# A two-layer graph network on one core: a form of its own for the last group, and other places for the first loads and norms

## The chip, the cores and the metric

The kernel runs on one core of a Trainium2 chip. A core has TensorE (matrix products), VectorE (DVE in the profile), ScalarE (ACT), GpSimd (POOL) and SyncE (SP). DMA transfers are issued from the instruction streams of ACT, SP and GpSimd and carried out by sixteen DMA engines. The metric is the device time of one execution in microseconds. The kernel before takes 2562.37 us, the median of three runs (2562.05 to 2563.6).

## The reference

Input `x` is 128 batches of 128 nodes with 512 features, all in float32. Two layers follow one another. Reduced to what is computed:

```python
# layer 0
h = relu(layernorm(x))
q, k, v = h @ Wq.T, h @ Wk.T, h @ Wv.T            # 512 x 512 each
rel = adj.T * (q @ k.T)                           # per batch, 128 x 128
rel = rel / norm(rel, axis=2, keepdims=True)
x = x + rel @ v
# layer 1: 8 heads of 64 columns
h = relu(layernorm(x))
q, k, v = h @ Wq + bq, h @ Wk + bk, h @ Wv + bv
s = q_head @ k_head.T / 8 + where(adj == 0, -1e9, 0)
x = x + concat(softmax(s) @ v_head)
```

## The kernel before

The 128 batches are worked in 32 groups of four (`G = 4`). `Layer0(g)` and `Layer1(g)` hold the two layers of group g. A dense product takes the four batches together: 512 rows by 512 features against a 512 x 512 weight. `Product` (L196) does it by Strassen's way, in seven products of half size, P1 to P7, each of which is four matmuls of 256 columns into one PSUM bank (the profile counts each float32 matmul as two passes, so eight). P1, P5 and P6 end in a copy out of PSUM (L227), P2, P3 and P7 in an addition on DVE (L243), P4 in a copy into the result. The sums of inputs that this needs are `sumA` and `sumB` (L349, L360), the sums of weights are made once (`sums`, L91).

Layer 0 is arranged so that it needs two dense products instead of three: `weights0` (L118) makes Wq' Wk once on TensorE (L124) and copies it out (L115, L116), the product G turns `h` with it (`pg`), `R` (L383) is the relation, `mask_rel` and `square` (L392, L398) mask and square it, `N` and `norms` (L403 to L411) give the norm, `V` (`pv0`) the values, and `O` and `xO` (L415, L421) add the result to `x`. Layer 1 has the dense products Q, K and V, with biases; the scores of one batch, all heads, are `S` (L446); `mk` adds the mask and takes the maximum (L455, L457); `ex` is eight exponentials on ACT with their sums (L464); `A` (L492) is the attention output, with the head's 64 columns as weights, so that it comes out turned (features in the partitions); `oc` copies it out (L503).

Matrices are turned in two ways. The usual one goes through DRAM: `send_blocks` (L182) writes a tile to DRAM in blocks of 32 from ACT's queue, `fetch_blocks` (L188) reads it back with four DMAs from SP's queue so that the blocks lie turned, and DVE turns the inside of each 32 x 32 block. For the norm `h` the three steps are `hn`, `rd` and `T` (L296 to L317), for the exponentials `ex`, `wr` and `wt` (L459 to L482), for the attention output `oc`, `rdo` and `ot` (L499 to L528). `ot` also scales by the reciprocal sums (L520), adds to `x` on GpSimd (L527) and writes the batch out from GpSimd's queue (L528). The other way is on TensorE, with the identity: `hn_pe` and `turn_pe` (L319 to L337), used for group 0 only.

The layernorm is `stat` on DVE (L284, L285), `inv` on GpSimd (four small operations for two batches, L291 to L294) and `hn` on ACT with scale and bias. In each group the two halves of two batches are handled apart: `stat0`, `stat1` and `inv0` serve `hn0`, and so on.

Buffers that matter here: `xpool` 12 tiles of `x`; `npool` ("e", for `hn`, `e` and `oT`) 3; `tpool` ("u", what was read back) 2; `wpool` ("wT") 3; `work` ("o") 2; in PSUM `ps_mm` 4 banks for the products, `ps_s` one double bank for the scores, `ps_o` two banks for everything else.

The order of the work is written out by hand. Under `manual_schedule` (L579) every engine runs its instructions in the order in which the program calls them, and the calls come from strings of steps which `run` (L566) walks through: `FIRST` for group 0, `SECOND` for group 1, `ORDER` for groups 2 to 31, and `LAST` after them. In a step the letter names the object: `m` is layer 0 of the current group, `n` layer 1 of the same group, `f` layer 0 of the next one, `l` and `p` layer 1 of the one before and of the one before that; `w` holds the weights of layer 1. So the pass of group g also carries layer 1 of group g - 1, and `LAST` carries what remains: the last group's Q, K, S, V and A, and the end of the one before.

What comes ahead of the strings (L73 to L74, L98 to L106 and L580 to L592) is the head: the loads of `x` of group 0 from SP's queue (four of 256 KB), of the raw weights of layer 0 from ACT's queue (four pieces of `raw_q` and `raw_k` in turn, 256 KB each, then `raw_v`), then statistics, the loads of group 1 and of layer 1's weights from GpSimd's queue (`load1`, L145, twelve DMAs, of which three carry biases), the turned norm of group 0, `weights0` and `weights_v0`. Of the steps that follow, `w.scale` (L162 to L164) multiplies layer 1's Q weights by 1/8 on ACT.

## Time and profile before

| What | Value |
|---|---|
| median of the runs | 2562.37 us |
| the profiled execution, its own time | 2561.42 us |
| its span, first to last instruction | 2559.6 us |
| PE busy | 2509.3 us, 98% |
| DVE busy | 1714.1 us, 67% |
| ACT busy | 1022.0 us, 40% |
| POOL (GpSimd) busy | 538.1 us, 21% |
| moved by DMA | 409.90 MB, mean 160 GB/s |
| exponentials to DRAM, `d_w<-e` | 128 DMAs of 512 KB, 2.6 us from issue to landing |
| their way back, `u_w<-d_w` | 512 DMAs of 128 KB, 2.9 us |
| attention output to DRAM, `d_o<-oT` | 64 DMAs of 512 KB, 4.2 us |
| its way back, `u_o<-d_o` | 256 DMAs of 128 KB, 3.3 us |

Times in the trace count from the start of the span. In the timeline a line gives the start, the length, the engine and the line of the code, the operation with its tiles and shapes, and in square brackets the idle time before it and what ended it; `x8` means that eight alike instructions stand in one line. An engine's name with a small q is its instruction queue issuing a DMA. In the view by windows a line gives the stretch, then its length, the busy time of PE, PE's weight loads, DVE, ACT and POOL (each with its number of instructions), and at the end three numbers: the clock that TensorE was granted (1.00 is full), the mean busy share of the DMA engines, and GB/s. In the chain of what ended last a line gives start and length of one step; the next line is what it released.

### The profile page before, as it was taken

How to read it: one execution, taken by the hardware profiler on the slowest of the kernel's cores; microseconds unless marked ns; L12 is line 12 of the kernel's file. 1: busy time of each engine (PE TensorE's matmuls, PEld its weight loads, DVE VectorE, ACT ScalarE, POOL GpSimd, SP SyncE). 2: the span in 40 equal slices, each digit the busy share in tenths (PEclk: the TensorE clock that was granted, in tenths of full speed). 3: DMA queues.
4: the chain of work that ended last, by engine and by line, in shares of the span. 5: the costliest groups of instructions: out<-in, count | busy, mean ns of one | idle time of the engine just before them, and what ended most of it. 6: DMA issues, size and time to landing. Idle time of an engine off the chain costs nothing.

```text
span 2559.6 us, 40828 instructions
## 1 busy us (share of the span) xinstructions
PE 2509.3 (98%) x14656; PEld 2131.7 (83%) x14656; DVE 1714.1 (67%) x2485; ACT 1022.0 (40%) x3248; POOL 538.1 (21%) x950
## 2 busy tenths in 40 slices
PE   8999999999999999999999999999999999999994
PEld 5788888888888888888888888888888888888883
DVE  5476766666766667666667666676666767666664
ACT  2344434444433334433444434444334344333442
POOL 4111222122122212122212121111221121222111
PEclk9999999999999999999999999999999999999997
DMA  4255444556444555445555445554445554445543
GB/s 170 83 168 178 161 152 141 181 161 194 152 143 153 179 165 190 146 141 166 173 173 171 152 147 168 169 184 157 148 149 173 165 192 149 146 157 176 162 140 132
DMA packets 374380, 409.90 MB, mean 160 GB/s; under 512 B 29921, under 2 KB 290145, under 8 KB 374177
## 3 DMA queue, kind: packets, MB, share of 16 engines
q1 hardware_dynamic: 281168, 167.92, 23.3%
q10 hardware_dynamic: 71792, 169.89, 17.9%
q0 software_dynamic: 21216, 69.49, 7.6%
q8 instruction: 115, 1.88, 0.3%
q14 instruction: 89, 0.72, 0.1%
HBM read 206.90 MB, written 200.28 MB: 159 GB/s over the span
## 4 chain that ended last, share of the span: by engine, by line
PE 96%; DVE 1%; DMA 1%; ACT 1%; issue 0%; POOL 0%; SPq 0%; ACTq 0%; POOLq 0%; DVEq 0%
PE pv_x L219 17%; PE pq_x L219 9%; PE pv_z L219 9%; PE pk_x L219 9%; PE pg_x L219 9%; PE pss L446 5%; PE po L492 5%; PE pr L383 4%; PE pv_y L219 4%; PE pg_z L219 4%; PE po L415 4%; PE pk_z L219 4%; PE pq_z L219 4%; PE pq_y L219 2%; PE pk_y L219 2%; PE pg_y L219 2%
## 5 line engine op out<-in xcount | busy, mean ns | idle before, releaser
L464 ACT ACTIVATE e<-pss,nmax 128x128 f32<-128x128 f32 x1024 | 359.7, 379 | 202.3 <-DVE nmax L457 180.1
L527 POOL TENSOR_TENSOR xb<-xb,o 128x512 f32<-128x512 f32 x128 | 163.3, 1276 | 1159.3 <-DVE o L520 1157.8
L219 PE MATMUL pv_x<-wc_v,h 128*128 128x256 f32 x1280 | 300.9, 382 | 0.7 <-DVE pv_r L236 0.7
L219 PEld LDWEIGHTS pv_x<-wc_v,h 128*128 128x128 f32 x1280 | 240.4, 190 | 51.6 <-DVE v L243 11.7
L302 ACT ACTIVATE hn<-xb,shift,rstd 128x512 f32<-128x512 f32 x252 | 190.9, 807 | 172.2 <-POOL shift L294 167.4
L219 PE MATMUL pv_z<-wc_v,s 128*128 128x256 f32 x1024 | 245.1, 382 | 0.0
L464 ACT ACTIVATION_READ_ACCUMULATOR e<-pss,nmax 128x1 f32 x1024 | 224.1, 219 | 0.0
L455 DVE TENSOR_TENSOR pss<-pss,mask 128x1024 f32<-128x1024 f32 x128 | 157.1, 1228 | 97.1 <-PE pss L446 97.1
L219 PEld LDWEIGHTS pv_z<-wc_v,s 128*128 128x128 f32 x1024 | 192.1, 190 | 28.5
L314 DVE STREAM_TRANSPOSE h<-u_h 128x1024 f32<-128x1024 f32 x126 | 156.4, 1241 | 86.1 <-DMA u_h<-d_h 78.2
L219 PE MATMUL pv_x<-wc_v,s 128*128 128x256 f32 x768 | 184.9, 384 | 0.0
L219 PE MATMUL pq_x<-h,wc_q 128*128 128x256 f32 x768 | 184.7, 383 | 0.0
L219 PE MATMUL pk_x<-h,wc_k 128*128 128x256 f32 x768 | 181.5, 379 | 0.0
L284 DVE BATCH_NORM_STATS2 st<-xb 128x6 f32<-128x512 f32 x256 | 172.0, 672 | 4.6 <-DMA xb<-in_x_dram 4.6
L446 PEld LDWEIGHTS pss<-kT,qT 64*128 64x128 f32 x2048 | 124.3, 187 | 49.4 <-PE po L415 23.5
L291 POOL TENSOR_SCALAR rstd<-mv 128x2 f32<-128x2 f32 x128 | 28.4, 221 | 650.3 <-DVE mv L285 650.3
L219 PEld LDWEIGHTS pq_x<-h,wc_q 128*128 128x128 f32 x768 | 143.4, 190 | 23.4 <-ACT oT L503 5.1
L219 PEld LDWEIGHTS pk_x<-h,wc_k 128*128 128x128 f32 x768 | 145.9, 190 | 19.9
L479 DVE STREAM_TRANSPOSE wT<-u_w 128x1024 f32<-128x1024 f32 x128 | 152.8, 1194 | 10.4 <-DMA u_w<-d_w 10.4
L457 DVE TENSOR_REDUCE nmax<-pss 128x8 f32<-128x1024 f32 x128 | 156.7, 1224 | 4.4
L219 PEld LDWEIGHTS pv_x<-wc_v,s 128*128 128x128 f32 x768 | 140.8, 190 | 20.4 <-DVE pv_r L236 0.2
L446 PE MATMUL pss<-kT,qT 64*128 64x128 f32 x2048 | 149.0, 285 | 3.1 <-ACT e L464 2.9
(134 smaller groups left out, 4440.4 us busy)
## 6 DMA issues: line engine op xcount, KB each, us to landing
d_w<-e ACTq DMA_DIRECT2D x128, 512.0 KB, 2.6
u_w<-d_w SPq DMA_DIRECT2D x512, 128.0 KB, 2.9
d_h<-hn ACTq DMA_DIRECT2D x126, 512.0 KB, 3.5
u_h<-d_h SPq DMA_DIRECT2D x504, 128.0 KB, 3.2
d_o<-oT ACTq DMA_DIRECT2D x64, 512.0 KB, 4.2
u_o<-d_o SPq DMA_DIRECT2D x256, 128.0 KB, 3.3
out_dram<-xb POOLq DMA_DIRECT2D x128, 256.0 KB, 2.9
xb<-in_x_dram POOLq DMA_DIRECT2D x124, 256.0 KB, 3.2
```

What stands on the lines that cost most here:

```text
L219: nc.tensor.matmul(ps[:, m, :], lhsT=lhsT, rhs=rhs, start=first and m == 0 and k == 0, stop=k == 1, skip_group_check=True,)
L284: nc.vector.bn_stats(st, x_tiles[g, b])
L302: nc.scalar.activation(hn[:, r], x_tiles[g, b].rearrange("p (k j q) -> p j k q", j=TB, q=BK), AF.Relu, bias=self.shift[:, b : b + 1], scal ...
L314: nc.vector.transpose(half.rearrange("p k (t i) -> p t k i", i=BK), self.u.pop(i).rearrange("p t (k q) -> p t k q", q=BK),)
L383: nc.tensor.matmul(pr[:, b, :], lhsT=self.turned(k, b), rhs=self.gT[:, k, ts(b, P)], start=(k == 0), stop=(k == KD - 1),)
L446: nc.tensor.matmul(pss[:, r, k, :], lhsT=self.qT[rows, k, ts(b, P)], rhs=self.kT[rows, k, ts(b, P)], start=True, stop=True,)
L455: nc.vector.tensor_tensor(sc, sc, mask[:, None, :].to_broadcast([P, H, P]), ALU.add)
L457: nc.vector.tensor_reduce(self.nmax[b], sc, AX.X, ALU.max, negate=True)
L464: nc.scalar.activation(e[:, :, i, :], sc[:, i, :].rearrange("p (j q) -> p j q", q=BK), AF.Exp, bias=nmax[:, i : i + 1], accum_out=self.tot ...
L479: nc.vector.transpose(self.wT[b].rearrange("p h (t i) -> p t h i", i=BK), self.uw.pop(b).rearrange("p t (h q) -> p t h q", q=BK),)
L492: nc.tensor.matmul(po[r * HD : (r + 1) * HD, k, :], lhsT=self.v[:, b, ts(2 * k + r, HD)], rhs=wT[:, r * NH + k, :], start=True, stop=True,)
L527: nc.gpsimd.tensor_tensor(xb, xb, o.rearrange("p k t q -> p (k t q)"), ALU.add)
```

## The change

The change has two parts, which share no step.

**The head.** The four loads of group 0's `x` are issued from SP's queue behind `raw_k`, which itself moves from ACT's queue to SP's; `raw_q` stays on ACT's. The object `f` (layer 0 of group 1) is made before `weights0`, and its statistics (`f.stat` for four batches, on DVE) and `f.inv0`, `f.inv1` (on GpSimd) stand right behind `m.hn_pe(1)`, ahead of the copies of `pa` on DVE and behind the DMA issues of group 1's loads and of `load1` on GpSimd. In `FIRST` these steps are gone; `f.hn0 f.rd0` stand right behind `m.G.P1`, `w.scale` behind `m.G.P5`, `m.V.P4` ahead of `n.hn0`, `n.hn1 n.rd1` behind `f.G.P5` and `n.T0` behind `f.G.P7`.

**The last group.** `LAST` is new from `l.Q.P3` on. `p.A1 p.oc1 p.rdo1` stand behind `l.S1 l.mk1`. Batches 0 and 1 of the last group keep the exponentials' way through DRAM. Batches 2 and 3 have `mk` and `ex` in halves of four heads (`mkA`, `mkB`, `exA`, `exB`); `e` is written in plain order and turned on TensorE by `tw` (eight transposes into two PSUM tiles of `ps_o`, each copied out on ACT). All four batches have their attention output from `An`: eight matmuls with the turned exponentials as weights and 64 columns of `v` as the moving side, so that it comes out with the nodes in the partitions. `fin` multiplies it by the reciprocal sums on DVE, adds it to `x` (on GpSimd, for batch 3 on DVE) and writes it out from SP's queue. For this group there is no `oc`, `rdo` and `ot`. `p.ot1`, the end of the group before, stands between `fin1` and `fin2`.

```diff
...
         queue.dma_start(xb, x[g * G + b])
         x_tiles[g, b] = xb
-    for b in range(G):
-        load(0, b, nc.sync)
     ident = const.tile([P, P], F32, tag="ident", name="ident")
     make_identity(nc, ident)
...
     for name, w, tag in (("q", wq0, "pq"), ("k", wk0, "pk"), ("v", wv0, "pv0")):
         raw[name] = ppool.tile([P, KD, D], F32, tag=tag, name=f"raw_{name}")
     for k in range(KD):
-        for name, w in (("q", wq0), ("k", wk0)):
-            nc.scalar.dma_start(raw[name][:, k, :], w[ts(k, P), :])
+        for name, w, queue in (("q", wq0, nc.scalar), ("k", wk0, nc.sync)):
+            queue.dma_start(raw[name][:, k, :], w[ts(k, P), :])
+    for b in range(G):
+        load(0, b, nc.sync)
     nc.scalar.dma_start(raw["v"], wv0.rearrange("(k p) d -> p k d", p=P))
     adj_sb = const.tile([P, P], F32, tag="adj", name="adj_sb")
     nc.sync.dma_start(adj_sb, adj)
...
             self.kT = ppool.tile([P, NH, G * P], F32, tag="pk", name=f"kT_{g}")
             self.Q = Product(self, "q", self.qT, True, bq_sb, name=f"pq_{g}")
             self.K = Product(self, "k", self.kT, True, bk_sb, name=f"pk_{g}")
-            self.rs, self.wT, self.ps, self.nmax, self.po = {}, {}, {}, {}, {}
+            self.rs, self.wT, self.ps, self.nmax, self.po, self.e = {}, {}, {}, {}, {}, {}
             self.dw, self.uw, self.total, self.do, self.uo = {}, {}, {}, {}, {}
         def start_v(self):
...
                 self.wT[b].rearrange("p h (t i) -> p t h i", i=BK),
                 self.uw.pop(b).rearrange("p t (h q) -> p t h q", q=BK),
             )
+        def mk_r(self, b, r):
+            sc = self.ps[b][:, r * NH : (r + 1) * NH, :]
+            nc.vector.tensor_tensor(sc, sc, mask[:, None, :].to_broadcast([P, NH, P]), ALU.add)
+            if r == 0:
+                self.nmax[b] = small.tile([P, H], F32, tag="nmax", bufs=2, name=f"nmax_{self.g}_{b}")
+            nc.vector.tensor_reduce(
+                self.nmax[b][:, r * NH : (r + 1) * NH], sc, AX.X, ALU.max, negate=True
+            )
+        def ex_r(self, b, r):
+            g, sc, nmax = self.g, self.ps[b], self.nmax[b]
+            if r == 0:
+                self.total[b] = small.tile([P, H], F32, tag="total", bufs=4, name=f"total_{g}_{b}")
+                self.e[b] = npool.tile([P, H, P], F32, tag="e", name=f"en_{g}_{b}")
+            for i in range(r * NH, (r + 1) * NH):
+                nc.scalar.activation(
+                    self.e[b][:, i, :], sc[:, i, :], AF.Exp,
+                    bias=nmax[:, i : i + 1], accum_out=self.total[b][:, i : i + 1],
+                )
+        def tw(self, b):
+            g = self.g
+            self.wT[b] = wpool.tile([P, H, P], F32, tag="wT", name=f"wT_{g}_{b}")
+            for r in range(2):
+                pt = ps_o.tile([P, NH, P], F32, tag="po", name=f"pw_{g}_{b}_{r}")
+                for k in range(NH):
+                    nc.tensor.transpose(pt[:, k, :], self.e[b][:, r * NH + k, :], ident)
+                nc.scalar.copy(self.wT[b][:, r * NH : (r + 1) * NH, :], pt)
+            self.rs[b] = small.tile([P, H], F32, tag="rs", bufs=8, name=f"rs_{g}_{b}")
+            nc.vector.reciprocal(self.rs[b], self.total.pop(b))
+        def An(self, b):
+            po, wT = ps_o.tile([P, D], F32, tag="po", name=f"pn1_{self.g}_{b}"), self.wT.pop(b)
+            for r in range(2):
+                for k in range(NH):
+                    i = 2 * k + r
+                    nc.tensor.matmul(
+                        po[:, ts(i, HD)], lhsT=wT[:, r * NH + k, :], rhs=self.v[:, b, ts(i, HD)],
+                        start=True, stop=True,
+                    )
+            self.po[b] = po
+        def fin(self, b):
+            g, xb = self.g, x_tiles.pop((self.g, b))
+            o = work.tile([P, D], F32, tag="o", name=f"o_{g}_{b}")
+            nc.vector.tensor_tensor(
+                o.rearrange("p (k r d) -> p k r d", k=NH, r=2),
+                self.po.pop(b).rearrange("p (k r d) -> p k r d", k=NH, r=2),
+                self.rs.pop(b).rearrange("p (r k) -> p k r", r=2)[:, :, :, None].to_broadcast(
+                    [P, NH, 2, HD]
+                ),
+                ALU.mult,
+            )
+            (nc.vector if b == G - 1 else nc.gpsimd).tensor_tensor(xb, xb, o, ALU.add)
+            nc.sync.dma_start(out[g * G + b], xb)
...
         def A(self, i):
...
     FIRST = """
-        m.sumA m.sumB m.start m.G.P1 w.scale m.G.P2 f.stat0 f.stat1 f.inv0 m.G.P5 f.hn0 f.rd0 m.G.P6 w.sumq
-        m.G.P3 f.stat2 f.stat3 f.inv1 m.V.P1 f.hn1 f.rd1 w.sumv m.G.P7 m.V.P2 w.sumk m.G.P4 m.V.P5
+        m.sumA m.sumB m.start m.G.P1 f.hn0 f.rd0 m.G.P2 m.G.P5 w.scale m.G.P6 w.sumq m.G.P3 m.V.P1 f.hn1 f.rd1
+        w.sumv m.G.P7 m.V.P2 w.sumk m.G.P4 m.V.P5
         m.R m.mask_rel m.square f.T0 m.V.P6 m.V.P3 m.N m.norms m.V.P7 m.O0 m.xO0 m.O1 m.xO1 n.stat0 n.stat1
-        n.inv0 n.hn0 n.rd0 m.V.P4 f.T1 m.O2 m.O3 f.sumA f.start f.G.P1 m.xO2 m.xO3 n.stat2 n.stat3 n.inv1
-        n.hn1 n.rd1 f.G.P2 f.sumB f.G.P5 f.G.P6 f.G.P3 n.T0 f.G.P7 f.G.P4 n.T1 n.start
+        n.inv0 m.V.P4 n.hn0 n.rd0 f.T1 m.O2 m.O3 f.sumA f.start f.G.P1 m.xO2 m.xO3 n.stat2 n.stat3 n.inv1
+        f.G.P2 f.sumB f.G.P5 n.hn1 n.rd1 f.G.P6 f.G.P3 f.G.P7 n.T0 f.G.P4 n.T1 n.start
     """.split()
     SECOND = """
         l.Q.P1 l.sumA l.Q.P2 l.sumB l.K.P1 l.K.P2 l.Q.P5 l.Q.P6 f.load0 f.load1 l.Q.P3 l.K.P5 l.K.P6 l.Q.P7
...
         l.wr3 l.V.P3 l.V.P7 n.T0 l.A0 l.oc0 l.V.P4 n.T1 n.start
     """.split()
     LAST = """
-        l.Q.P1 p.rdo0 l.sumA l.Q.P2 l.sumB l.K.P1 l.K.P2 p.wt3 l.Q.P5 p.ot0 l.Q.P6 l.Q.P3 p.A1 p.oc1
-        p.rdo1 l.K.P5 l.K.P6 l.Q.P7 l.K.P3 l.S0 l.mk0 l.K.P7 l.Q.P4 l.ex0 l.wr0 l.K.P4 l.S1 l.mk1 p.ot1
-        l.start_v l.V.P1 l.V.P2 l.ex1 l.wr1 l.V.P5 l.S2 l.mk2 l.V.P6 l.ex2 l.wr2 l.V.P3 l.wt0 l.V.P7 l.S3 l.mk3
-        l.V.P4 l.ex3 l.wr3 l.wt1 l.A0 l.oc0 l.rdo0 l.wt2 l.wt3 l.A1 l.oc1 l.rdo1 l.ot0 l.ot1
+        l.Q.P1 p.rdo0 l.sumA l.Q.P2 l.sumB l.K.P1 l.K.P2 p.wt3 l.Q.P5 p.ot0 l.Q.P6 l.Q.P3 l.K.P5 l.K.P6 l.K.P3
+        l.Q.P7 l.S0 l.mk0 l.K.P7 l.Q.P4 l.ex0 l.wr0 l.K.P4 l.S1 l.mk1 p.A1 p.oc1 p.rdo1 l.start_v l.V.P1
+        l.ex1 l.V.P2 l.V.P5 l.S2 l.mkA2 l.mkB2 l.V.P6 l.exA2 l.exB2 l.wt0 l.wr1 l.V.P3 l.V.P7 l.S3 l.mkA3 l.mkB3
+        l.tw2 l.wt1 l.exA3 l.exB3 l.V.P4 l.An0 l.fin0 l.An1 l.fin1 p.ot1 l.tw3 l.An2 l.fin2 l.An3 l.fin3
     """.split()
     def run(order, **who):
...
         load1()
         m.hn_pe(0)
         m.hn_pe(1)
+        f = Layer0(1)
+        for b in range(G):
+            f.stat(b)
+        f.inv(0)
+        f.inv(1)
         weights0(lambda: m.turn_pe(0))
         m.turn_pe(1)
         weights_v0()
         for g in range(NG):
             n = Layer1(g)
-            f = Layer0(g + 1) if g + 1 < NG else None
+            if g:
+                f = Layer0(g + 1) if g + 1 < NG else None
             run((FIRST, SECOND, ORDER)[min(g, 2)], p=p, l=l, m=m, n=n, f=f, w=Weights1())
             p, l, m = l, n, f
         run(LAST, p=p, l=l)
```

More of the change, by code (lines that the diff above doesn't have):

```diff
@@ L484, in A, with mkA, mkB, exA @@
+        def mkA(self, b):
+            self.mk_r(b, 0)
+        def mkB(self, b):
+            self.mk_r(b, 1)
+        def exA(self, b):
+            self.ex_r(b, 0)
+        def exB(self, b):
+            self.ex_r(b, 1)
         def A(self, i):
```

## The prediction

> **What bounds the kernel now.** First the page's engine shares and the line of 40 slices, to see whether any engine is full and where it is not:
>
> ```profile
> PE 2509.3 (98%) x14656; PEld 2131.7 (83%) x14656; DVE 1714.1 (67%) x2485; ACT 1022.0 (40%) x3248; POOL 538.1 (21%) x950
> ...
> PE   8999999999999999999999999999999999999994
> ```
>
> TensorE is the bound; only the first and the last slice are open. Taking the start of each group's first Q product from the timeline, groups 1 to 31 follow each other every 77.57 us (one 77.63), with no TensorE wait in between. So whatever moves the head moves the end by the same amount, and there are two places to look: before group 0's Q (at 85.55 us) and after the last dense product. The head, from the TensorE and ACT timelines:
>
> ```profile
> 34.41 1.89 PE L219 MATMUL pv_x<-wc_v,h 128*128 128x256 f32 x8
> 41.31 3.56 PE L219 MATMUL pg_x<-s,wc_a 128*128 128x256 f32 x8 [5.00 <-ACT pg_r L227]
> ...
> 61.37 1.89 PE L219 MATMUL pv_x<-wc_v,h 128*128 128x256 f32 x8
> 68.67 3.77 PE L415 MATMUL po<-v,rel 128*128 128x512 f32 x4 [5.41 <-ACT v L227]
> ```
> ```profile
> 38.64 1.52 ACT L302 ACTIVATE hn<-xb,shift,rstd 128x512 f32<-128x512 f32 x2 [6.90 <-POOL shift L294]
> ...
> 66.02 1.52 ACT L302 ACTIVATE hn<-xb,shift,rstd 128x512 f32<-128x512 f32 x2 [9.93 <-POOL shift L294]
> 67.56 0.37 ACTq L185 DMA_DIRECT2D d_h<-hn  x1
> 68.03 0.58 ACT L227 COPY v<-pv_x 128x512 f32<-128x512 f32 x1 [0.49 <-ACT hn L302]
> ```
>
> Both TensorE stalls have one form: TensorE needs a small ACT copy (`pg_r`, `v`), and that copy stands in ACT's queue behind a norm (`hn`) which waits for GpSimd's `shift`. After each stall the products run at half speed (3.56 instead of 1.89 for eight), and the windows view shows the granted clock (the first of the last three numbers) fall with it; the last row is the tail:
>
> ```profile
> 40.00:50.00 10.00, 8.69 (x32) 7.33 (x33) 6.08 (x9) 3.34 (x6) 6.01 (x8) 0.83 0.45 157
> 60.00:70.00 10.00, 4.59 (x14) 2.72 (x13) 6.21 (x10) 2.10 (x3) 1.73 (x4) 0.77 0.14 54
> 2530.00:2540.00 10.00, 3.68 (x32) 2.91 (x29) 3.03 (x4) 1.17 (x2) 0.23 (x1) 0.50 0.57 171
> ```
>
> The tail, from the chain that ended last (start, length, what):
>
> ```profile
> 2528.24 2.60 DMA d_w<-e
> ...
> 2532.30 3.29 DMA u_w<-d_w
> ...
> 2537.21 1.99 PE po L492 x16
> 2539.22 0.59 ACT oT L503
> 2539.83 2.70 DMA d_o<-oT
> ...
> 2543.95 3.12 DMA u_o<-d_o
> ...
> 2552.47 0.58 POOLq L625
> ```
>
> The exponentials (`d_w`, `u_w`) and then the output (`d_o`, `u_o`) each go through DRAM to be turned: write, four issues, read, about 7.5 us each time.
>
> **The head, step by step.** By queue: raw_k goes to SP beside raw_q on ACT, and x(0) behind raw_k. The Trainium skill (DMA: Bandwidth & Descriptors, "Issuing engines are not separate DMA queues") says that a second issuing queue saves only issue time, as all share 16 engines. That speaks against any gain here: with doubled bandwidth x(0) would be in by about 9. The trace agrees with the rule: the first eight transfers (2 MB) landed by 8.58 from two queues, and from one queue 256 KB then took 0.65 each. So x(0), now after 2 MB of weights and sharing with raw_v, lands at 9.8 to 13.7 instead of 4.6 to 8.2. Then statistics 0.9, `inv` 1.6 on GpSimd: to 16.2 (was 10.8). What is late next is x(1), queued on GpSimd behind that `inv`: issue to landing 3.0 for the first (median of these loads on the page 3.2; 3.8 here under load), then 0.55 to 0.65 each: 19.2 to 21.1. The added `f.stat` of four tiles (about 0.8 each) now stand on DVE ahead of the copies of `pa`: done at 22.5. The copies started at 20.78 before. 8 x 0.43 gives 26.0, and the transposes of raw_v, which wait for them, let the first G product begin at 26.4 (25.78 before): **+0.6**. TensorE itself starts at about 4.9 (6.14 before) and has done pa and the turns by 22.9, so it is not what binds.
>
> `f.inv` on GpSimd stands behind sixteen DMA issues (12.0 long before, of which 1.2 waits): 16.2 + 11 = 27.2, done 28.9 and 30.4. `f.hn0` runs on ACT 28.9 to 30.4, right after G.P1's copy; the P5 copy is due only at 31.8, so ACT holds nobody. `w.scale` (2.3) then ends at 34.7 and G.P6's copy at 35.3; G.P7 needs it at 36.8. The 5.00 stall and its half-clock product (3.35 between starts instead of 1.73) go. Ten products of 1.727 from 26.4 put R at 43.7 (50.00 before): **-6.3** so far.
>
> R to V.P4's end is 13.2 by its rows. V.P4's copy now precedes `n.hn0` on ACT: 0.16 drain, 0.1 and 0.58, so O2 starts at 57.7 (68.67): 4.7 more. O2 and O3 at full clock take 1.73 rather than 3.57: 1.8 more. From there six G products, the wait for P7's addition (0.85, stays), G.P4: Q.P1 at 72.6 instead of 85.55. **Head: -12.9.**
>
> What could now be late: `n.hn1` has moved behind G.P5's copy (65.4), so hn1's write is issued at 67.0. Its write took 6.23 before (x(2) loads were in flight; 2.75 alone), the read 4.0, the turn and sum 2.0: ready at 79.3; Q.P5 wants it at 79.5. The cover is 0.2, and beyond it each us late costs one. x(2) loads still go off just before, so the 6.2 stands. The T0 chain ends at about 71.7, under Q.P1's 72.6.
>
> Clock: the skill (TensorE: Matmul & The Clock Gate, Parts 1 and 4) says that about 3.4 us of idling halve the clock and that transposes do not count as busy. Between 22.9 and 26.4 TensorE has only raw_v's transposes (1.75). The rows show half clock after idles of 5.0 and 5.4, none after 2.0 (at 2506.67). By the rule the head would lose 1.7 more (-11.2), by the rows nothing; I take the rows, and the other for the range.
>
> **The tail, step by step** (before's time, the head's shift left out). Without p.A1 (1.9) between the products, Q.P4 starts at 2498.3 and ex0 runs 2500.9 to 2503.8, 2.8 earlier; S1 2503.9; p.A1 2505.0; V.P1, P2, P5 to 2512.1. ex1 has ended by 2511.0, behind p.oc1's copies, so S2 starts at once (2513.48 before). The head halves: mask 128x512 like the 0.69 of L392, reduction the same (half of L457's 1.22 plus its fixed part; between 0.61 and 0.75). Four in a row take 2.9 where two took 2.5: +0.4, and in the built order the exponentials wait for the second half's maximum, so halving hides nothing. ex2 2516.3 to 2519.2, S3 2519.2, the eight turns at 0.109 (row of L336) to 2521.2, V.P4 to 2523.0. An is not in the trace: sixteen passes of 64 columns on 128-column weights. Below it lies L492, 0.9 for 64-column weights; the nearest row is L403, 0.11 a pass with full weights and one column: 1.75. I take 1.7; at half clock up to 3.4. An0 to 2524.7. wT1's read waits for wT0's buffer, since u_o of the previous group holds the other: SP 2518.3, landed 2522.8, turned after mk3 at 2524.9. An1 to 2526.7; ex3 2523.4 to 2526.3; tw3 to 2528.1, copies 0.58; An2 2529.8, An3 2531.5.
>
> Next the moved p.ot1. It takes 2.8 of DVE and, on GpSimd, two additions (1.27) with two DMA issues (0.30 + 0.56) between fin1 and fin2, and both `o` buffers. GpSimd: fin0, fin1 to 2529.0, p.ot1 to 2533.5, fin2 to 2534.8. fin3's multiply waits for the last `o` buffer (2532.6), its addition is on DVE (to 2534.0). SP issues the last two rows by 2535.7, landing at 2538 (2.3 to 2.6). The program's end followed the last GpSimd issue by 7.1 before (2552.5 to 2559.6): from the issue at 2532.9 that gives 2540.0, from fin2's end 2541.9. I take 2541. **Tail: -18.6** (-15 to -20.5). Two DRAM trips, 15 us, and the last GpSimd row are gone; p.ot1 gives some 3 back.
>
> The sum is against the profiled execution: span 2559.6 - 12.9 - 18.6 = 2528.1, execution 2561.42 - 31.5 = 2529.9; the median of the runs lies 0.95 above that execution, so 2562.37 - 31.5 = **2531**.
>
> **Rivals.** *Head eaten by late data* (0.14): loads at 0.8 instead of 0.65 per 256 KB, or hn1's write queued wholly behind x(2), hold G.P1 and Q.P5 some 3 to 6 longer: head -8, 2536. For it: two covers under 1 us. *Tail held by GpSimd and cold clock* (0.10): An at 3.4 and `o` buffers in turn: tail -13, 2537. *More than the sum* (0.07): G.P1 at 25.5 and an end without GpSimd's trail: 2525. *The change does nothing, as the stalls move* (0.02): both ACT copies again behind norms: the head and the tail's gain would both have to fail. *Slower* (0.03): one window of 3.41 at half clock in every group costs 1.7 x 31 = 53, 2584; it decides from 1.05 lost per group (31.5 / 30). Against it: no TensorE wait in any group, and groups 1 to 30 keep their orders and their waits. *My forecast* (0.64).
>
> **How the numbers follow.** The likeliest case spans 2527 to 2535. The first two rivals end at about 2540, the faster one at 2524; with these the range holds the 8 in 10. About 0.2% (5 us) is what can be told from no change: faster needs a sixth of the sum, 0.95; same 0.02; slower 0.03.
>
> **What would show it.** Right: no wait for ACT at 36 and 63; granted clock 1.00 between 30 and 80; Q.P1 near 72.6; no `d_w` and `d_o` of the last two batches; about 55 us from the last group's Q.P1 to the end of the last An (62.7 before: 2476.5 to 2539.2), and p.ot1's two additions between fin1 and fin2 on GpSimd. Wrong: a DVE wait for xb longer than to 21, a TensorE wait for `h` or `s` at group 0's Q.P5, or group times other than 77.57.

## The result, and the profile after

The changed kernel takes 2538.26 us (median of five runs, 2536.59 to 2540.92), the kernel before 2562.37 in the same comparison: a ratio of 0.9907, with a 95% interval of 0.9892 to 0.9921. That is 24.1 us less; the forecast was 31.5 less. The profiled execution, which is the median run, has a span of 2536.5, so 23.1 below the 2559.6 of before and 8.4 above the 2528.1 that the prediction's sum gave.

The page of the changed kernel, its engine shares and the lines of 40 slices:

```profile
PE 2512.7 (99%) x14672; PEld 2135.8 (84%) x14672; DVE 1707.5 (67%) x2484; ACT 1023.9 (40%) x3248; POOL 535.0 (21%) x945
...
PE   8999999999999999999999999999999999999998
...
PEclk9999999999999999999999999999999999999999
```

The last slice, which was 4 before, is now 8: the end is filled with matrix work. The start of each group's first Q product splits the span into three. Before, group 0's came at 85.55, the last group's at 2476.5, and 83.1 us followed. Now they come at 76.75 and 2469.5, and 67.0 us follow. So the head gave 8.8, of which 1.7 was lost again inside group 0; the groups after it follow each other every 77.57 as before; and the tail gave 16.1. The head in the timeline of TensorE (start, length, what, and in brackets the idle time before it and what ended it):

```profile
25.20 3.31 PE L139 MATMUL pwv<-ident,raw_v 128*128 128x128 f32 x16 [2.53 <-issue]
28.30 2.62 PE L218 MATMUL pg_x<-h,wc_a 128*128 128x256 f32 x8
...
44.22 1.99 PE L218 MATMUL pg_x<-h,wc_a 128*128 128x256 f32 x8 [1.22 <-DVE gT L242]
...
61.71 1.98 PE L414 MATMUL po<-v,rel 128*128 128x512 f32 x4 [0.68 <-ACT v L226]
...
76.75 1.89 PE L218 MATMUL pq_x<-h,wc_q 128*128 128x256 f32 x8
...
84.83 1.99 PE L218 MATMUL pq_z<-s,wc_q 128*128 128x256 f32 x8 [1.02 <-DVE qT L242]
```

The two stalls that the prediction set out to remove are gone: 5.00 us ahead of `pg_x<-s` is nothing, and 5.41 ahead of the second `po` is 0.68. But four smaller losses have come: 2.53 ahead of the turns of raw_v (`pwv`), which then take 3.31 instead of 1.91; a first G product of 2.62; 1.22 ahead of G.P4; and 1.02 ahead of Q.P5. The windows (length, busy time of PE, weight loads, DVE, ACT, POOL; then granted clock, DMA share, GB/s):

```profile
20.00:30.00 10.00, 7.39 (x34) 5.43 (x33) 8.62 (x22) 3.66 (x10) 8.69 (x13) 0.83 0.97 336
...
40.00:50.00 10.00, 8.78 (x50) 7.66 (x50) 7.76 (x9) 2.76 (x5) 5.25 (x4) 1.00 0.33 105
...
60.00:70.00 10.00, 9.32 (x39) 7.14 (x38) 8.91 (x17) 3.74 (x6) 4.03 (x9) 1.00 0.20 72
...
2490.00:2500.00 10.00, 8.00 (x52) 6.83 (x52) 3.97 (x4) 4.48 (x20) 0.00 (x0) 0.88 0.13 53
```

The clock is whole where it had fallen (40 to 50, 60 to 70) and falls at two other places: 20 to 30, and 2490 to 2500. At the end the chain shows what has taken the place of the trip of the output through DRAM:

```profile
2526.81 1.28 POOL xb L597
...
2528.12 0.70 DVE o L531
...
2528.84 1.95 DVE xb L539
```

GpSimd's addition for `p.ot1` (L597) holds an `o` buffer, then DVE multiplies the last batch and adds it in 1.95 us.

### The profile page after: what moved, and what is told of

The parts are those of the page before. It is cut to its first block, busy times and chain, and to the rows that moved or that the text cites. A ratio compares the mean times of both kernels' runs of the same rounds, so it can differ in the third digit from the quotient of the medians.

```text
span 2536.5 us, 40820 instructions
## 1 busy us (share of the span) xinstructions
PE 2512.7 (99%) x14672; PEld 2135.8 (84%) x14672; DVE 1707.5 (67%) x2484; ACT 1023.9 (40%) x3248; POOL 535.0 (21%) x945
## 3 DMA queue, kind: packets, MB, share of 16 engines
q1 hardware_dynamic: 278992, 167.92, 23.4%
## 4 chain that ended last, share of the span: by engine, by line
PE 97%; DVE 1%; DMA 1%; ACT 0%; issue 0%; POOL 0%; SPq 0%; ACTq 0%; DVEq 0%; POOLq 0%
PE pv_x L218 18%; PE pq_x L218 9%; PE pv_z L218 9%; PE pk_x L218 9%; PE pg_x L218 8%; PE pss L445 5%; PE po L562 5%; PE pv_y L218 5%; PE pg_z L218 4%; PE pq_z L218 4%; PE pr L382 4%; PE pk_z L218 4%; PE po L414 4%; PE pk_y L218 2%; PE pg_y L218 2%; PE pq_y L218 2%
## 5 line engine op out<-in xcount | busy, mean ns | idle before, releaser
L597 POOL TENSOR_TENSOR xb<-xb,o 128x512 f32<-128x512 f32 x124 | 158.2, 1276 | 1103.6 <-DVE o L590 976.4
```

The lines of the kernel that those rows point to most:

```text
L597: nc.gpsimd.tensor_tensor(xb, xb, o.rearrange("p k t q -> p (k t q)"), ALU.add)
```

## The experiments

The theory after reading the two traces: the change does what it says, and the missing 8 us are four separate losses, each with its own cause: (1) group 0's `x` behind 2 MB of weights, and the clock that falls in the idle time which that makes; (2) DVE slowed by GpSimd's additions ahead of G.P4; (3) a PSUM bank that is freed late, ahead of Q.P5; (4) idle time ahead of S1 in the last group, and half clock after it. The rivals: the parts act on each other (the head changes what the tail meets); the loads are bound by the DMA engines, so that no other order helps; every repair only uncovers the next wait.

### One part alone

The first run has the order `LAST` of before, the second the head and `FIRST` of before.

> The new head with the old last group. By the difference of the two profiled executions the new head is worth 6.9 us at the last group's first Q product (2476.5 to 2469.6), and the old tail then runs as it did before, 83.1 us from there to the end: span about 2552.7, 6 to 7.5 below before. The prediction on record gave the head 12.9 (2547). If the two parts help each other (the end of the head changing what the tail meets), the sum of this run and the one with the tail alone will miss the 23 to 24 of both together by more than 2.

> The old head with the new last group. From the last group's first Q product the changed kernel needs 66.9 us where before needed 83.1: span about 2543.4, 16.2 below before; the prediction on record gave 18.6. Where the wait for S1 falls decides whether the clock is halved after it: full clock throughout would give 1.9 more, 18.

Measured: the head alone 2555.82 us, 0.9976 (0.9965 to 0.9987) of before's 2562.02; the tail alone 2543.97, 0.9929 (0.9914 to 0.9944). That is 6.2 and 18.1, together 24.3, and both parts together gave 24.1: the parts add up. The tail's profiled execution beat its expectation by 0.7 (span 2542.7) since the clock stayed whole in it; from its last group's first Q product it needed 65.4 us, not 67.0.

### Where the head's gain lies

```diff
-        n.inv0 m.V.P4 n.hn0 n.rd0 f.T1 m.O2 m.O3 f.sumA f.start f.G.P1 m.xO2 m.xO3 n.stat2 n.stat3 n.inv1
+        n.inv0 n.hn0 n.rd0 m.V.P4 f.T1 m.O2 m.O3 f.sumA f.start f.G.P1 m.xO2 m.xO3 n.stat2 n.stat3 n.inv1
```

> The changed kernel with one step of FIRST moved back: m.V.P4 behind n.hn0 n.rd0 as before. V.P4's copy on ACT then stands behind the norm that waits for GpSimd's shift: the copy comes at about 65.8 instead of 61.1, O2 starts at 66.4 instead of 61.7, with some 5 us of idle TensorE ahead of it and half clock after it. First Q product at 82 to 83 (75.1 to 78.3 with this head in three executions), of which 1 is given back at Q.P5; the whole 4 to 5.5 us longer than the changed kernel, about 2543. If the copy's place is not what the head gains from, under 1.

Measured: 2542.12 us, 3.9 above the changed kernel's median. TensorE's timeline has the old stall back, half clock after it included:

```profile
68.07 3.78 PE L414 MATMUL po<-v,rel 128*128 128x512 f32 x4 [5.35 <-ACT v L226]
```

The first Q product came at 85.31, later than the 82 to 83 expected, since G.P4 and the product behind it ran at half clock in this execution. Group 0 was 1.6 shorter, as the wait at Q.P5 was gone. So the first Q product came 7 to 10 later than in the other runs with the changed kernel's head, and where it came before the change (85.55). The time says the same: 0.9922 of before, beside 0.9929 with the tail alone, which differ by less than the noise. Without this one copy's move, what the other edits of the head win at the first stall goes to the losses that they bring. No run moves this copy alone in the old head, so what it gives by itself is not shown.

### Group 0's loads

```diff
     for k in range(KD):
         for name, w, queue in (("q", wq0, nc.scalar), ("k", wk0, nc.sync)):
             queue.dma_start(raw[name][:, k, :], w[ts(k, P), :])
-    for b in range(G):
-        load(0, b, nc.sync)
+        for b in range(2 * k, min(2 * k + 2, G)):
+            load(0, b, nc.sync)
```

> The changed kernel with SP's first issues in another order: raw_k 0, x 0 and 1, raw_k 1, x 2 and 3, raw_k 2 and 3. My reading of the changed kernel is that x of group 0 behind 2 MB of weights makes everything that follows it late (inv1 ends at 16.8 instead of 10.8, x of group 1 lands to 23.3, the statistics end at 24.4 where the copies of pa could start at 20.8), and that TensorE's 2.5 us without work then halves its clock. So here inv1 ends at about 11, the statistics by 19, the copies start as pa ends, G.P1 starts at 24.4 to 25.0 (28.3 in the changed kernel) at full clock, and the first Q product at 72 to 73 (76.75): 4 us less. The rival is that the 16 DMA engines are the limit: raw_k then comes later by what x gains, pa ends about 2 us later, and G.P1 starts no earlier than 27.

Measured: 2533.67 us, 0.9889 (0.9875 to 0.9904) of before. TensorE's timeline:

```profile
21.71 2.66 PE L139 MATMUL pwv<-ident,raw_v 128*128 128x128 f32 x16
24.20 1.89 PE L218 MATMUL pg_x<-h,wc_a 128*128 128x256 f32 x8
...
31.93 1.99 PE L218 MATMUL pg_z<-s,wc_a 128*128 128x256 f32 x8 [0.66 <-ACT pg_r L226]
...
41.59 3.55 PE L218 MATMUL pg_x<-h,wc_a 128*128 128x256 f32 x8 [2.49 <-DVE gT L242]
```

G.P1 starts at 24.20, without idle time ahead of the turns and at full clock. The rival of the DMA engines falls: raw_k's last piece landed at 13.5 instead of 8.5, and yet `pa` ended at 20.9 instead of 21.8. But the first Q product is only 0.9 earlier than in the changed kernel, not 4. G.P3 (31.93) waits for P5's copy, which now comes late behind `f.hn0`: GpSimd's `f.inv0` ended at 29.28, just ahead of the product P5 (29.55), and `hn0` then held ACT:

```profile
29.31 1.52 ACT L301 ACTIVATE hn<-xb,shift,rstd 128x512 f32<-128x512 f32 x2 [2.59 <-POOL shift L293]
...
31.29 0.59 ACT L226 COPY pg_r<-pg_z 128x512 f32<-128x512 f32 x1 [0.46 <-PE pg_x L218]
```

And G.P4's wait has grown to 2.49, and that product runs at half clock (3.55). (The time is 4.6 below the changed kernel's median. Of the 2.6 between the two profiled executions 0.9 comes from the head and 1.6 from the tail, whose clock stayed whole here.) The rival "it uncovers the next wait" holds here until loss 2 and the place of `f.hn0` are mended too.

### DVE beside GpSimd

```diff
-        w.sumv m.G.P7 m.V.P2 w.sumk m.G.P4 m.V.P5
-        m.R m.mask_rel m.square f.T0 m.V.P6 m.V.P3 m.N m.norms m.V.P7 m.O0 m.xO0 m.O1 m.xO1 n.stat0 n.stat1
+        m.G.P7 m.V.P2 w.sumk m.G.P4 m.V.P5
+        m.R m.mask_rel m.square f.T0 m.V.P6 m.V.P3 m.N m.norms w.sumv m.V.P7 m.O0 m.xO0 m.O1 m.xO1 n.stat0 n.stat1
```

> The changed kernel with w.sumv, four additions on GpSimd, moved from behind hn1 to behind m.norms; nothing on DVE is moved. In the changed kernel the four DVE instructions of w.sumq take 1.00, 1.64, 1.77 and 1.75 while GpSimd adds, where the same on w.sumk takes 0.69 as soon as GpSimd is done; they hold G.P3's addition and so G.P4 by 1.2 us (2.5 and then half clock in the kernel with x between). If GpSimd's additions slow DVE's, then those of sumq that start after GpSimd's sums of v0 take 0.69, sumq ends at least 1.5 us earlier, and G.P4 does not wait; first Q product 1.4 to 3 earlier than with the same head. If they are slow for themselves, nothing changes at G.P4.

First the changed kernel's DVE: three of `w.sumq`'s four, the addition of G.P3 that they hold, and two of `w.sumk`'s, of which the first still meets GpSimd's last addition (it ends at 45.3) and the second does not:

```profile
37.96 1.64 DVE L91 TENSOR_TENSOR wc_q<-wc_q 128x512 f32<-128x512 f32 x1
39.52 1.77 DVE L92 TENSOR_TENSOR wc_q<-wc_q,w_q 128x512 f32<-128x512 f32 x1
41.21 1.75 DVE L93 TENSOR_TENSOR wc_q<-wc_q 128x512 f32<-128x512 f32 x1
42.89 0.68 DVE L242 TENSOR_TENSOR gT<-pg_z,pg_r 128x512 f32<-128x512 f32 x1
...
44.69 1.18 DVE L90 TENSOR_TENSOR wc_k<-w_k,wc_k 128x512 f32<-128x512 f32 x1
45.91 0.69 DVE L91 TENSOR_TENSOR wc_k<-wc_k 128x512 f32<-128x512 f32 x1
```

Then the four of `w.sumq` in the run with `w.sumv` moved, where GpSimd's last sum of v0 runs from 38.0 to 39.8:

```profile
37.96 0.69 DVE L90 TENSOR_TENSOR wc_q<-w_q,wc_q 128x512 f32<-128x512 f32 x1 [3.48 <-ACT w_q L162]
38.69 1.64 DVE L91 TENSOR_TENSOR wc_q<-wc_q 128x512 f32<-128x512 f32 x1
40.25 0.68 DVE L92 TENSOR_TENSOR wc_q<-wc_q,w_q 128x512 f32<-128x512 f32 x1
40.85 0.68 DVE L93 TENSOR_TENSOR wc_q<-wc_q 128x512 f32<-128x512 f32 x1
```

The same instructions, on the same tiles, take 0.68 once GpSimd is silent and 1.64 beside it. G.P4 did not wait, and V.P2 to R took 5.18 instead of 6.67. The additions out of PSUM (42.89, with GpSimd busy) kept their 0.68. The Trainium skill (SBUF — State Buffer, "SBUF: two separate sides") names a cause: GpSimd and DVE share a pair of SBUF ports, held as a lock for a whole instruction, and a DVE instruction with two inputs in SBUF needs it beside a GpSimd one that reads SBUF. The rows agree with it, and GpSimd is slowed too: its addition beside these took 1.79 instead of 1.28. The lock itself stands in no row. The whole was 2535.52 us. Its profiled execution, the longest of the four, reached the first Q product only at 77.21: it had 4.19 us idle ahead of raw_v's turns, with half clock behind them, and lost 1.0 there against the changed kernel, and 0.9 in a new wait for `h` ahead of Q.P1.

### The bank ahead of Q.P5

```diff
-        f.G.P2 f.sumB f.G.P5 n.hn1 n.rd1 f.G.P6 f.G.P3 f.G.P7 n.T0 f.G.P4 n.T1 n.start
+        f.G.P2 f.sumB f.G.P5 n.hn1 n.rd1 f.G.P6 f.G.P3 f.G.P7 n.T0 f.G.P4 n.start
...
-        l.Q.P1 l.sumA l.Q.P2 l.sumB l.K.P1 l.K.P2 l.Q.P5 l.Q.P6 f.load0 f.load1 l.Q.P3 l.K.P5 l.K.P6 l.Q.P7
+        l.Q.P1 l.Q.P2 l.T1 l.sumA l.sumB l.K.P1 l.K.P2 l.Q.P5 l.Q.P6 f.load0 f.load1 l.Q.P3 l.K.P5 l.K.P6 l.Q.P7
```

> The changed kernel with n.T1 of group 0 moved from FIRST into SECOND behind Q.P2, so that on DVE Q.P2's addition comes ahead of the turn of the second half, not behind it and sumA. In the changed kernel Q.P5 waits 1.02 us: not for s, which is ready at 83.45, but for a PSUM bank, which that addition frees at 84.78. If that is so, Q.P5 follows K.P2 with no more than 0.2 us of wait, and the first group takes 64.3 instead of 65.45. If s was what was late, nothing is won.

Measured: Q.P5 (`pq_z`) follows K.P2 (`pk_y`) without a wait:

```profile
80.10 1.89 PE L218 MATMUL pk_y<-h,wc_k 128*128 128x256 f32 x8
81.83 1.89 PE L218 MATMUL pq_z<-s,wc_q 128*128 128x256 f32 x8
```

Group 0 takes 63.72 us instead of 65.45, as it did before the change. The time was 2536.6: 1.7 below the changed kernel, as it should be, but less than the runs of that kernel differ among themselves.

### The hole ahead of S1

```diff
-        l.Q.P7 l.S0 l.mk0 l.K.P7 l.Q.P4 l.ex0 l.wr0 l.K.P4 l.S1 l.mk1 p.A1 p.oc1 p.rdo1 l.start_v l.V.P1
+        l.Q.P7 l.S0 l.mk0 l.K.P7 l.Q.P4 l.ex0 l.wr0 l.K.P4 p.A1 p.oc1 p.rdo1 l.S1 l.mk1 l.start_v l.V.P1
```

> The changed kernel with p.A1, p.oc1, p.rdo1 ahead of S1 instead of behind it. In the changed kernel TensorE has nothing for 2.0 us ahead of S1 and then runs S1 and p.A1 at half clock (1.65 and 3.02 instead of 1.1 and 1.9). If the idle 2.0 us halves the clock, p.A1 in that hole keeps the clock at 1.00 from 2490 to 2510, and V.P1 starts 3.4 us earlier after the last group's first Q product (32.1 us in the changed kernel, 28.7 here); the end comes 3 to 3.5 us earlier. If the clock falls for another reason, only the 1.9 of the hole are gained.

TensorE in the changed kernel, S1, p.A1 and V.P1:

```profile
2497.09 1.65 PE L445 MATMUL pss<-kT,qT 64*128 64x128 f32 x16 [2.00 <-ACT e L463]
2498.67 3.09 PE L562 MATMUL po<-wT,v 128*64 128x128 f32 x32
2501.69 1.99 PE L218 MATMUL pv_x<-wc_v,h 128*128 128x256 f32 x8
```

and with p.A1 in the hole:

```profile
2496.70 1.97 PE L562 MATMUL po<-wT,v 128*64 128x128 f32 x32
2498.76 1.16 PE L445 MATMUL pss<-kT,qT 64*128 64x128 f32 x16
2499.86 1.99 PE L218 MATMUL pv_x<-wc_v,h 128*128 128x256 f32 x8
```

V.P1 came 28.7 us behind the last group's first Q product, as expected, the clock stayed whole, and the end came at 63.8 instead of 67.0. The median, 2537.12, is only 1.1 lower; in the profiled execution the head was 1.5 later at the first Q product, and 1.5 of the 3.2 are left at the end.

The other runs tell more about this hole than the one made for it. It is there, 2.0 us long, in ten of the profiles. In five of them (before, the tail alone, x between, V.P4 back, the output turned) S1 took 1.16 and the clock stayed whole; in five (the changed kernel, the head alone, sumv later, Q.P2 first, the exponentials in DRAM) the clock fell, at S1 or at what follows it. So 2.0 us of idle time halve the clock in some executions and not in others, for 1.6 us (65.4 or 67.0 to the end in the kernels whose tail is the changed one's). The Trainium skill (TensorE: Matmul & The Clock Gate, Part 1, "What's actually happening") says that activity is judged in windows of 3.4 us that run freely, and that the clock falls after an idle one. The profiles show such windows: in each of them the granted clock changes only on a grid of 3.41 us, and the grid lies differently in every run. In the five profiles in which the clock fell, the whole hole lies in one window of the grid, in which TensorE was busy for 1.41 to 1.45 us. In the other five an edge of the grid cuts the hole, no window is left with less than 1.51, and the clock stays whole. The window with the hole and the one behind it, in the changed kernel and then with the tail alone:

```profile
2494.19:2497.60 3.41, 1.41 (x13) 0.96 (x13) 0.00 (x0) 2.94 (x18) 0.00 (x0) 1.00 0.01 2
2497.60:2501.01 3.41, 3.41 (x34) 3.19 (x34) 2.14 (x2) 1.07 (x3) 0.00 (x0) 0.50 0.43 163
...
2503.31:2506.72 3.41, 1.83 (x30) 1.71 (x32) 0.57 (x1) 2.36 (x12) 0.00 (x0) 1.00 0.31 129
2506.72:2510.13 3.41, 3.41 (x34) 2.99 (x30) 2.11 (x3) 2.23 (x9) 0.00 (x0) 1.00 0.46 132
```

So where the hole falls decides, as the page has it; but the window need not be idle throughout, since 1.45 us of work in it were too little. Ahead of G.P4 the border is about the same: windows with 1.53 or less were followed by half clock, those with 1.71 or more were not. (With only An to do, at the very end, up to 2.5 us of work were too little; why, no run tells.) Ahead of raw_v's turns, six profiles have a window with 0.40 to 1.07 us of work, and the clock fell in all six, after 2.53 us of idle time or more. With 1.87 or less it stayed whole, also where a window held nothing but 2.07 or 2.10 us of these turns (Q.P2 first, the head alone).

### Which half of the new last group pays

The exponentials of batches 2 and 3 through DRAM:

```diff
-        l.ex1 l.V.P2 l.V.P5 l.S2 l.mkA2 l.mkB2 l.V.P6 l.exA2 l.exB2 l.wt0 l.wr1 l.V.P3 l.V.P7 l.S3 l.mkA3 l.mkB3
-        l.tw2 l.wt1 l.exA3 l.exB3 l.V.P4 l.An0 l.fin0 l.An1 l.fin1 p.ot1 l.tw3 l.An2 l.fin2 l.An3 l.fin3
+        l.ex1 l.V.P2 l.V.P5 l.S2 l.mk2 l.V.P6 l.ex2 l.wt0 l.wr1 l.V.P3 l.V.P7 p.ot1 l.wr2 l.S3 l.mk3
+        l.wt1 l.ex3 l.wr3 l.V.P4 l.An0 l.fin0 l.An1 l.fin1 l.wt2 l.An2 l.fin2 l.wt3 l.An3 l.fin3
```

> The last group with its attention output in rows (An, fin) as in the changed kernel, but with the exponentials of batches 2 and 3 turned through DRAM as before (whole mk and ex, wr, wt), and p.ot1 behind V.P7, since a read-back buffer comes free only with it. By the rows of the changed kernel: p.ot1 to 2518.4, mk3 to 2520.9, ex3 to 2524, the write to 2526.7, the read to 2530, the turn to 2531.3, An3 to 2533.2, its row at 2534.7 instead of 2530.8: 3.5 to 4 us longer, a span of about 2540. The rival: with the output in rows the way of the exponentials through DRAM is hidden, and the span stays within 1 of 2536.5.

The output turned:

```diff
-        l.tw2 l.wt1 l.exA3 l.exB3 l.V.P4 l.An0 l.fin0 l.An1 l.fin1 p.ot1 l.tw3 l.An2 l.fin2 l.An3 l.fin3
+        l.tw2 l.wt1 l.exA3 l.exB3 l.V.P4 l.A0 l.oc0 p.ot1 l.rdo0 l.tw3 l.A1 l.oc1 l.rdo1 l.ot0 l.ot1
```

> The changed kernel with the exponentials of batches 2 and 3 turned on TensorE as in it, but the last group's attention output as before: turned (A), copied (oc), through DRAM (rdo) and turned back (ot), with p.ot1 behind oc0. By the rows: A1 ends at 2526, oc1's copies at 2527.3, the write at 2530, the read at 2534, ot1 on DVE and GpSimd at 2538 to 2539 and the last row out by 2545: 8 to 10 us longer than the changed kernel, about 2547. With the 5.0 of the run that kept the exponentials in DRAM these make up the 16 to 18 of the tail only if A1, S1 and the end of the previous group bring the rest; if this run is under 5 longer, the row form of the output is not where the tail's gain lies.

Measured: 2543.5 us with the exponentials in DRAM, 2550.22 with the output turned. To the end they need 71.95 (beside the 67.0 of the changed kernel, both with the clock fallen) and 76.46 (beside 65.4, both with it whole): 4.9 and 11.0. TensorE in the first of them, the last two outputs:

```profile
2526.09 3.65 PE L522 MATMUL pn<-v,wT 128*128 128x64 f32 x16 [2.15 <-DVE wT L478]
2531.89 3.65 PE L522 MATMUL pn<-v,wT 128*128 128x64 f32 x16 [2.15 <-DVE wT L478]
```

Each waits for the turn of what came back from DRAM, and each takes 3.65 instead of 1.8: waiting brings the half clock with it, which the 3.5 to 4 had left out. The output in rows is the larger half. Together they are 15.9 of the 17.7 by which the tail gets shorter where its clock stays whole (83.1 to 65.4); the rest, p.A1's place and the end of the group before among it, no run separates.

### All repairs together

The first of three, against the run with `x` between:

```diff
-        m.sumA m.sumB m.start m.G.P1 f.hn0 f.rd0 m.G.P2 m.G.P5 w.scale m.G.P6 w.sumq m.G.P3 m.V.P1 f.hn1 f.rd1
-        w.sumv m.G.P7 m.V.P2 w.sumk m.G.P4 m.V.P5
-        m.R m.mask_rel m.square f.T0 m.V.P6 m.V.P3 m.N m.norms m.V.P7 m.O0 m.xO0 m.O1 m.xO1 n.stat0 n.stat1
+        m.sumA m.sumB m.start m.G.P1 w.scale m.G.P2 m.G.P5 f.hn0 f.rd0 m.G.P6 m.G.P3 m.V.P1 f.hn1 f.rd1
+        m.G.P7 m.V.P2 w.sumq w.sumk m.G.P4 m.V.P5
+        m.R m.mask_rel m.square f.T0 m.V.P6 m.V.P3 m.N m.norms w.sumv m.V.P7 m.O0 m.xO0 m.O1 m.xO1 n.stat0 n.stat1
...
-        f.G.P2 f.sumB f.G.P5 n.hn1 n.rd1 f.G.P6 f.G.P3 f.G.P7 n.T0 f.G.P4 n.T1 n.start
+        f.G.P2 f.sumB f.G.P5 n.hn1 n.rd1 f.G.P6 f.G.P3 f.G.P7 n.T0 f.G.P4 n.start
...
-        l.Q.P1 l.sumA l.Q.P2 l.sumB l.K.P1 l.K.P2 l.Q.P5 l.Q.P6 f.load0 f.load1 l.Q.P3 l.K.P5 l.K.P6 l.Q.P7
+        l.Q.P1 l.Q.P2 l.T1 l.sumA l.sumB l.K.P1 l.K.P2 l.Q.P5 l.Q.P6 f.load0 f.load1 l.Q.P3 l.K.P5 l.K.P6 l.Q.P7
...
-        l.Q.P7 l.S0 l.mk0 l.K.P7 l.Q.P4 l.ex0 l.wr0 l.K.P4 l.S1 l.mk1 p.A1 p.oc1 p.rdo1 l.start_v l.V.P1
+        l.Q.P7 l.S0 l.mk0 l.K.P7 l.Q.P4 l.ex0 l.wr0 l.K.P4 p.A1 p.oc1 p.rdo1 l.S1 l.mk1 l.start_v l.V.P1
```

> The changed kernel with all the repairs together: x of group 0 between the pieces of raw_k, w.scale back ahead of f.hn0 (which goes behind G.P5's copy), w.sumq behind V.P2's addition, w.sumv behind m.norms, Q.P2's addition ahead of T1, p.A1 ahead of S1. If the losses are what I take them for and lie one behind the other, G.P1 starts at 24.2, the first Q product at 70.5 to 71 (76.75 in the changed kernel) without a wait over 0.7 on the way but for O2's and G.P4's, the first group takes 63.7, and the end is 63.8 behind the last group's first Q product: a span of 2525.5, a time of 2527. If each repair only moves the wait to the next cover, the span stays above 2530.

The second, against the first:

```diff
-        l.ex1 l.V.P2 l.V.P5 l.S2 l.mkA2 l.mkB2 l.V.P6 l.exA2 l.exB2 l.wt0 l.wr1 l.V.P3 l.V.P7 l.S3 l.mkA3 l.mkB3
-        l.tw2 l.wt1 l.exA3 l.exB3 l.V.P4 l.An0 l.fin0 l.An1 l.fin1 p.ot1 l.tw3 l.An2 l.fin2 l.An3 l.fin3
+        l.ex1 l.V.P2 l.V.P5 l.S2 l.mk2 l.V.P6 l.exA2 l.exB2 l.wt0 l.wr1 l.V.P3 l.V.P7 l.S3 p.ot1 l.mk3
+        l.tw2 l.wt1 l.exA3 l.exB3 l.V.P4 l.An0 l.fin0 l.An1 l.fin1 l.An2 l.fin2 l.tw3 l.An3 l.fin3
```

> As combo_a, with the last group's mk whole again (2.45 instead of 2.88 for four halves), p.ot1 ahead of mk3 instead of between fin1 and fin2, and An2, fin2 ahead of tw3. By the rows of the changed kernel: mk3 and ex3 come 2.4 later, since p.ot1 takes 2.8 to 3.8 of DVE ahead of them, but An2 lies under them, the wait for po ahead of tw3's second half goes, and GpSimd and DVE have only fin2 and fin3 at the end, so that fin3's addition takes 0.7 instead of 1.95: the end 1 to 2 us earlier than combo_a. If p.ot1 on DVE delays the exponentials by more than the end gains, it is later, by up to 1.

Measured: the first 2529.14 us, 0.9872 (0.9857 to 0.9886) of before, 2 above its expectation: its copies of `pa` had to wait 1.1 us once more for the statistics (G.P1 at 26.08), so that the first Q product came at 72.65; in the second, which has the same head, they did not (24.22, and 70.76, in the middle of what was expected). In both, no wait over 0.8 is left between G.P1 and the first Q product. In the first, and again in the third below, one group in the middle took 1.0 to 1.1 longer, as one block of `h` came back from DRAM late (in the first at 524.1, 4.4 us after its issue, where the three ahead of it needed 2.3 to 2.6); what delayed it is not known. The second took 2530.7, and its gain at the end was not there (64.7 us against 64.2): p.ot1 ahead of `mk3` held `wt1` and so An1, TensorE was idle for 2.25, and the outputs ran at half clock.

The third, against the first:

```diff
-            (nc.vector if b == G - 1 else nc.gpsimd).tensor_tensor(xb, xb, o, ALU.add)
+            (nc.vector if b >= G - 2 else nc.gpsimd).tensor_tensor(xb, xb, o, ALU.add)
...
-                nc.gpsimd.dma_start(out[g * G + b], xb)
+                (nc.sync if (g, i) == (NG - 2, 1) else nc.gpsimd).dma_start(out[g * G + b], xb)
```

> As combo_a, with fin2's addition on DVE like fin3's, and the two rows of p.ot1 written out from SP's queue. In the changed kernel and in combo_a the span ends 6.25 us after GpSimd's last instruction (its closing drain takes 5.5 of them), though SP's last row is issued 5.3 us ahead of the end; in the two runs where GpSimd had finished early the end came 2.7 to 2.8 after SP's last issue. If the drain sets the end, GpSimd's last addition now ends 2.1 us earlier (no fin2 and no issues behind it) and the span ends 61.9 to 62.2 behind the last group's first Q product instead of 64.2; fin3's addition, with GpSimd idle beside it, takes 0.7 instead of 1.95. A time of 2527. If the rows' landing sets the end, it stays within 0.5 of 64.2.

What led to it is the end of the profiles. The last instruction of GpSimd and of DVE in the first of the three:

```profile
2521.70 1.27 POOL L539 TENSOR_TENSOR xb<-xb,o 128x512 f32<-128x512 f32 x1
```

```profile
2521.58 1.95 DVE L539 TENSOR_TENSOR xb<-xb,o 128x512 f32<-128x512 f32 x1
```

The span ends at 2529.2, which is 6.25 behind the end of GpSimd's last instruction (2522.97). In the changed kernel it is 2536.48 behind 2530.23, 6.25 again. And with the exponentials in DRAM, where GpSimd had ended 8.15 ahead of the end, the end came 2.7 behind SP's last issue. The last of DVE in the third:

```profile
2520.43 0.69 DVE L539 TENSOR_TENSOR xb<-xb,o 128x512 f32<-128x512 f32 x1
```

The last addition took 0.69 instead of 1.95, GpSimd's last instruction ended at 2519.25, and the span at 2525.4: 6.1 behind it, and 61.6 behind the last group's first Q product. The time is 2527.14 us, 0.9864 (0.9847 to 0.9880) of before: the fastest version here, 34.6 below before in its comparison, and 11 below the changed kernel by the two medians.

## Why the prediction was right and where it fell short

The direction, the two places and their mechanisms were right: both ACT stalls went (the head's gain hangs on the second, by the run with V.P4 moved back), and so did both trips through DRAM at the end. The size was not: 24.1 for 31.5. The 2538.26 lies outside the 2527 to 2535 of the likeliest case, and inside the range only because this takes in the ends of the two slower rivals. Each of these came true in part (the head lost 5.8 of its 12.9, the tail 2.5 of its 18.6); the prediction had no case for both at once, and that they stayed within the range is luck.

Of the signs named, the whole clock from 30 to 80 and the groups at 77.57 came; Q.P1 near 72.6 and about 55 us to the end of the last An did not (76.75 and 57.45). Two signs of being wrong came: DVE waited for `xb` until 22.75, and TensorE waited at Q.P5, though for a bank and not for `h` or `s`. In the profiled execution 8.4 of span are missing, and they are these.

**x(1) and the statistics.** The prediction had `f.stat` done at 22.5 and G.P1 at 26.4. The last tile landed at 23.4 (21.1 predicted), since the third came 2.2 behind the second; the statistics were done at 24.45, and since the copies then ran every 0.33 instead of 0.43, 1.1 of it reached G.P1. DVE's wait for the third tile, the last of its statistics and the first copy of `pa`:

```profile
22.75 0.69 DVE L283 BATCH_NORM_STATS2 st<-xb 128x6 f32<-128x512 f32 x1 [1.21 <-DMA xb<-in_x_dram]
...
24.27 0.18 DVE L284 BATCH_NORM_AGGREGATE mv<-st 128x2 f32<-128x6 f32 x1
24.38 0.39 DVE L114 COPY wc_a<-pa 128x256 f32<-128x256 f32 x1
```

"Then 0.55 to 0.65 each" was the mis-sized term. What held the third tile stays open; before, the fourth had come 1.7 behind the third.

**The clock, in the head.** "I take the rows, and the other for the range": this step failed. raw_v's turns and the first G product lost 1.5 in the profile; the rule that the prediction weighed there (idle time halves the clock, and transposes do not count as work) would have cost 1.7. The row that it took against the rule, "none after 2.0 (at 2506.67)", held by the place of that hole: an edge of the grid cut it, and no window was left with less than 2.1 us of work. But the rule is not what the runs show either. The turns did count as work: 2.07 and 2.10 us of them alone kept the clock whole, and in the run with V.P4 moved back a window with nothing else, full from 24.92 to 28.33, brought it back. What halved the clock in the changed kernel was that TensorE had 1.07 us of work between 22.93 and 26.35, as the copies of `pa` came late.

**A cover that held by luck.** `f.inv0` was to be done at 28.9 and was done at 31.13: the DMA issues ahead of it took 12.1 instead of 11, and its four operations 2.3 instead of 1.6. That cost nothing only because G.P1 was late as well. With the loads between, where G.P1 was in time, `hn0` held P5's copy and so G.P3 by 0.66.

**G.P4.** "Ten products of 1.727 from 26.4 put R at 43.7" took DVE's weight sums at 0.69. Beside GpSimd's they took up to 1.77, and G.P4 lost 1.4. The trace of before had shown it: DVE's sums at 28.5 to 33.4 took 1.64 to 1.75 there, while GpSimd added.

**Q.P5.** "Ready at 79.3; Q.P5 wants it at 79.5": `s` was ready in time (83.45 for 83.65, all 4 later), but the product also needed a bank, which Q.P2's addition freed at 84.78, behind the turn and `sumA` on DVE. That cost 1.2, and 0.5 more was lost behind it in group 0, 0.3 of it where `N` waited for `sq`.

**The tail.** An was sized well (1.83 for 1.7), and ex0 and S1 began within 0.3 of their places. The clock fell in the hole ahead of S1, 1.6, for which the same row "none after 2.0" had left nothing. The rest, 0.9, lies in p.ot1 and the end: p.ot1 took 3.9 of DVE for 2.8, its multiplications 1.2 beside GpSimd's additions, and of the two estimates of the end, 2540.0 and 2541.9, the second, from the end of GpSimd's last addition, was the right one in kind (it was 6.25 us from there, not 7.1); the prediction took a middle, 2541.

Together: 1.1 + 1.5 + 1.4 + 1.7 in the head, 1.6 + 0.9 in the tail, 8.2 of 8.4. The rivals "head eaten by late data" and "tail held by GpSimd and cold clock" each came true in part, and at the same time; each alone was given a smaller chance than the undisturbed sum.

## What to carry to other kernels

Ahead of a product that starts late, list every release that it needs, the PSUM bank among them, and what stands before each releasing instruction on its engine; a cover of 0.2 us counts only for the one that was looked at. When work is moved to GpSimd or beside it, DVE instructions with two inputs in SBUF are to be costed at two and a half times their row, as the trace shows. And a hole of 2 us on TensorE may cost nearly as much again in clock: fill it with work that is due anyway, before anything else is sought.

## What was not expected of the hardware

- The program's end waits for GpSimd: where GpSimd worked to the end the span ends 6.1 to 6.6 us behind its last instruction (twelve profiles), and 2.7 to 2.8 behind SP's last issue where GpSimd had ended early (two). GpSimd should be the first engine to finish.
- The same hole of 2.0 us halved the clock in five profiles of ten, those in which it lay within one window of 3.41 us. The head differs from run to run too: the same one reached its first Q product at 74.9 to 78.3 in six profiles. The changed kernel's runs spread over 4.3 us; those of before spread over 1.7 in that comparison, though over up to 3.7 in the others.
- A DVE addition of two SBUF tiles takes 0.69 alone and 1.64 to 1.77 beside a GpSimd addition; one that reads PSUM keeps its 0.68.
